# One PSUM region for a unit's scores, one product for the sum of its heads, and the src ids turned and sent by ScalarE

## The chip, the cores and the metric

The kernel runs on one core of one Trainium2 chip. Its time is in device microseconds, the median of several runs; lower is better. A core has five engines with an instruction queue each: PE (TensorE, matrix products, with PEld for the loading of its weights), DVE (VectorE), ACT (ScalarE), POOL (GpSimd) and SP (SyncE, which here only issues transfers). Each engine works through its own queue in order, and semaphores make an instruction wait for another engine or for a transfer.

## What is computed

One attention layer over a graph of 12,500 nodes and 412,500 edges, with residual and two layer norms. Cut to what matters:

```
h, q, k, v = x @ Wn + bn, x @ Wq + bq, x @ Wk + bk, x @ Wv + bv      # 12500 x 128
eh     = edge_attr @ We + be                                          # 412500 x 128
hmid   = leaky_relu(concat(q[src], k[dst], eh) @ A1 + b1, 0.2)        # 412500 x 128
scores = leaky_relu(hmid @ A2 + b2, 0.2)                              # 412500 x 8 heads
w      = softmax(scores.mean(axis=-1), axis=0)                        # over all edges
out    = segment_sum(w[:, None] * v[dst], src, 12500)
y      = layer_norm(h + out) * gamma + beta
result = layer_norm(x + y)
```

The edges come in sorted by dst. So k and v of neighbouring edges lie close together, while q and the sum go by src, which is in no order.

## The kernel before

All is in `sorted_path` (L456). Nodes are cut into blocks of 128, 98 of them, and edges into groups of 1024, 403 of them, which are dealt with in six parts (`CUTS`).

**Making** (`make`, L797, for each part). A group of edges becomes records of 260 floats: the row of v, the part of the hidden layer that comes from dst and from the edge's own attributes, and the src id. PE builds them by one-hot products (L914, L919), ScalarE takes them out of PSUM (L929, L930), and POOL scatters them to DRAM by src block with one indirect DMA per 128 records (L941, 3224 in all) into `rtab`.

**Sums** (`sums_of`, L1072). When a part is made, its records are read back, two src blocks at a time: a **unit**. There are 294, 49 for each part; those of parts 0, 4 and 5 have 12 tiles of 128 records, those of parts 1 to 3 have 14. What one unit goes through, by the functions' names:

- `load` (L1105, SP): the records, `rt`. `load_q` (L1117, SP): q of its two blocks, `qs`.
- `sources` (DVE, L1131): the src id of each record inside its block, `sl`, one column for each tile.
- `turn` (PE, L1139) transposes `sl` into PSUM, so that a tile's ids lie in a row; `turned` (DVE, L1146) takes them out as bytes, `slT`; `put` (L1153, SP) writes them to DRAM as `row`, 1.5 or 1.8 KB; `spread` (L1158, SP) reads them back to all 128 partitions, `rowB`, 192 or 224 KB.
- `onehot` (DVE, L1170): from `rowB` the one-hot matrix `ohT` that picks q. Four tiles are a piece, so this and the next three run three or four times a unit.
- `hidden` (PE, L1184 and L1193): `rt` transposed plus q picked by `ohT`, into PSUM, `ph`. `sloped` (ACT, L1204) writes 0.2 of it to `hm`, and `leaky` (DVE, L1208) the maximum of both.
- `scores` (PE, L1221): hm times A2. A product fills 32 partitions and up to 512 columns: three tiles side by side at 12 tiles, four at 14. Four products fill the four groups of partitions of one PSUM bank, `psc`.
- `above_zero` (ACT, L1235): a ReLU of scores plus b2, from PSUM to `z`, in one piece at 12 tiles and in two at 14. The leaky ReLU of a head is 0.8 of the ReLU plus 0.2 of the linear value; the sum over heads of the linear value is carried by two extra columns of `A2s`, one for its positive and one for its negative part.
- `heads` (PE, L1247): three or four products with `headsum`, which sum the heads of a record into one column for each tile, in `psm`.
- `maxima` (DVE), `maximum` (PE, L1268) and `reference` (DVE, L1276 and L1277): the largest score so far. `weights` (ACT, L1286): the exponentials, `w`, and their sum.
- `select` (DVE, L1295) and `weigh` (ACT, L1309): one-hot of src times w, `ohw`; `add` (PE, L1338): the sum by src; `total` (DVE, L1354): the earlier parts' sum, rescaled, plus this one; `lowered` (ACT, L1328 and L1331) keeps the reference; `store` (SP) writes it.

**What sets the order.** Nothing is reordered by a compiler. `lags` (L1044) and, for the last part, `last_lags` (L1060) give each function a step, as an offset from its unit's first product:

```
turned=-turn + 1 + e, spread=-turn + 3 + 2 * e, q=-9, onehot=-1 - e, sloped=1,
leaky=2, scores=L + 1, above=L + 2 + e, heads=L + 3 + 2 * e, maxima=f, maximum=f + 1,
```

L is twice the number of pieces. `do` files each function under its step, so that several units are in flight at once, and the loop at the end of `sorted_path` deals the steps of part p-1's units out evenly among the making of part p. The last part's units have nothing to be mixed with and run alone behind the making, from about 4440 us; the two layer norms (`closing`) follow from about 4840 us.

**Buffers.** `psc` has one PSUM bank, which the turned ids and the scores of all units take in turn (in the last part the ids have a bank of their own, `late["turn"]`). `z` has one buffer. A hardware DMA takes one of eight semaphores in turn, over all engines that issue any, and first waits for the DMA eight before it.

Of the kernel before, what the change touches and what calls it, by code (L numbers as in the profile page):

```python
# [455 lines left out]
def sorted_path(  # L456
# [39 lines left out]
    A2s = const.tile([D, 32], FP)  # L496
    nc.vector.memset(A2s, 0.0)
    nc.scalar.dma_start(out=A2s[:, :H], in_=A2)
    nc.vector.tensor_reduce(A2s[:, H : H + 1], A2s[:, :H], AX.X, ALU.add)
    for j, part in enumerate((1.0, -1.0)):  # L500
        nc.vector.tensor_scalar(
            A2s[:, H + 1 + j : H + 2 + j], A2s[:, H : H + 1], part * SLOPE / (1 - SLOPE), None,
            op0=ALU.mult,
        )
    nc.vector.memset(A2s[:, H : H + 1], 0.0)
    b2_r = const.tile([1, 32], FP)
    nc.vector.memset(b2_r, 0.0)
    nc.scalar.dma_start(out=b2_r[:, :H], in_=b2.rearrange("h o -> o h"))
    nc.vector.tensor_reduce(b2_r[:, H : H + 1], b2_r[:, :H], AX.X, ALU.add)
    for j, part in enumerate((1.0, -1.0)):  # L510
        nc.vector.tensor_scalar(
            b2_r[:, H + 1 + j : H + 2 + j], b2_r[:, H : H + 1], part * SLOPE / (1 - SLOPE), None,
            op0=ALU.mult,
        )
    nc.vector.memset(b2_r[:, H : H + 1], 0.0)
    b2_d = dram.tile([32, 1], FP, name="b2_d")
    nc.scalar.dma_start(out=b2_d.rearrange("h o -> o h"), in_=b2_r)
    b2_c = const.tile([P, 1], FP)
    headsum = const.tile([P, 4], FP)
    nc.vector.memset(headsum, 0.0)  # L520
    signs = const.tile([32, 1], FP)
    nc.gpsimd.memset(signs, 1 - SLOPE)
    nc.gpsimd.affine_select(
        out=signs, in_=signs, compare_op=ALU.not_equal, fill=SLOPE - 1, base=-(H + 2),
        pattern=[[0, 1]], channel_multiplier=1,
    )
    for j in range(4):
        nc.scalar.dma_start(out=b2_c[32 * j : 32 * j + 32, :], in_=b2_d)
        nc.vector.tensor_copy(headsum[32 * j : 32 * j + 32, j : j + 1], signs)
# [237 lines left out]
    zp_ = pool("z", 1)  # L767
# [6 lines left out]
    pscp = pool("psc", 1, space=PSUM)  # L774
# [269 lines left out]
    def lags(p, nk):  # L1044
# [3 lines left out]
        if p == NP - 1:  # L1048
# [5 lines left out]
            leaky=2, scores=L + 1, above=L + 2 + e, heads=L + 3 + 2 * e, maxima=f, maximum=f + 1,  # L1054
# [5 lines left out]
    def last_lags(nk):  # L1060
# [6 lines left out]
            heads=L + 5, maxima=f, maximum=f + 1, reference=f + 2 + e, weights=f + 3 + e,  # L1067
# [4 lines left out]
    def sums_of(bp):  # L1072
# [63 lines left out]
        def turn(i):  # L1136
            st, nt = state[i], plans[i][0]
            st["pT"] = late.get("turn", pscp).tile([P, 4 * P], FP, name="psc")
            nc.tensor.matmul(  # L1139
                st["pT"][:nt, :P], st["sl"][:, :nt], identB, start=True, stop=True  # L1140
            )

        def turned(i):
            st, nt = state[i], plans[i][0]
            st["slT"] = scp.tile([TM, P], U8, name="slT")
            nc.vector.tensor_scalar(  # L1146
                st["slT"][:nt, :], st.pop("pT")[:nt, :P], 0.0, None, op0=ALU.max
            )

        def put(i):  # L1150
            st, nt = state[i], plans[i][0]
            st["row"] = srow.tile([TM, P], U8, name="row")
            nc.sync.dma_start(out=st["row"][:nt, :], in_=st.pop("slT")[:nt, :])  # L1153

        def spread(i):
            st, nt = state[i], plans[i][0]
            st["rowB"] = late.get("row", rowp).tile([P, TM * P], U8, name="rowB")
            nc.sync.dma_start(  # L1158
# [52 lines left out]
        def slices(m):  # L1211
            sw = -(-m // 4)
            return sw, [(j, min(sw, m - j)) for j in range(0, m, sw)]

        def scores(i, t0, m):
            st = state[i]
            sw, sl = slices(m)
            hm = st["hm"].pop(t0)
            psc = pscp.tile([P, 4 * P], FP, name="psc")
            for q, (j, n) in enumerate(sl):  # L1220
                nc.tensor.matmul(  # L1221
                    psc[32 * q : 32 * q + 32, : n * P], A2s, hm[:, j * P : (j + n) * P],
                    start=True, stop=True,
                )
            full = sum(n == sw for _, n in sl)
            st["z"] = psc, [(0, 32 * full, sw)] + [
                (32 * q, 32 * q + 32, n) for q, (_, n) in enumerate(sl) if q >= full
            ]

        def above_zero(i):  # L1230
            st = state[i]
            psc, pieces = st["z"]
            st["z"] = z = zp_.tile([P, 4 * P], FP, name="z")
            for p0, p1, n in pieces:
                nc.scalar.activation(  # L1235
                    z[p0:p1, : n * P], psc[p0:p1, : n * P], AF.Relu, bias=b2_c[p0:p1, :]
                )

        def heads(i, t0, m):
            st = state[i]  # L1240
            sw, sl = slices(m)
            if t0 == 0:
                st["psS"] = psmp.tile([P, 4 * P], FP, name="psm")
            z = st.pop("z")
            for j in range(sw):
                nv = sum(n > j for _, n in sl)
                nc.tensor.matmul(  # L1247
                    st["psS"][:, t0 + j : t0 + j + (nv - 1) * sw + 1 : sw],
                    z[: 32 * nv, j * P : (j + 1) * P], headsum[: 32 * nv, :nv],
                    start=True, stop=True,  # L1250
                )
# [613 lines left out]
```

## Time and profile before

| | |
|---|---|
| median of 3 runs | 4985.54 us (4974.44 to 4991.73) |
| the profiled execution: its time, its span | 4977.97 us, 4976.3 us |
| PE, products (and weight loads) | 4076.9 us, 82% (64%) |
| DVE | 4181.3 us, 84% |
| ACT | 3168.0 us, 64% |
| POOL | 3327.3 us, 67% |
| DMA | 1462.23 MB, mean 294 GB/s |
| scatters of records (POOL L941) | 3224, 3242.7 us |
| granted TensorE clock, mean | 0.93 |

The busy shares are means over three very different stretches: making with sums (up to about 4440 us, its pace set by different engines early and late), the last part's sums alone, and the layer norms. PE and DVE are both over 80% busy and neither is so all the time, so a row of busy time says little by itself; what an engine waited for, inside one stretch, says more. In a row of a group the figures before the bar are the shape and the count, then come the busy time and the mean length in ns, then the idle time of that engine just before such an instruction and what ended it. In a row of waits stand the idle time, the number of waits and the longest one. In a row of the timeline stand the start, the length, the engine, the line and the operation.

### The profile page before, as it was taken

The page shows a single profiled execution, that of the slowest core. Times are in us where ns is not written, and L with a number is a line of the kernel's source. Part 1 is how long each engine was busy: PE and PEld are TensorE (multiplying, and loading weights), DVE is VectorE, ACT ScalarE, POOL GpSimd, SP SyncE. Part 2 cuts the span into 40 slices and gives each one's busy share as a digit, 9 for nine tenths or more (in the row PEclk, how much of TensorE's full clock was granted, in tenths as well). Part 3 has the DMA queues.
Part 4 walks back from the last instruction along what each step waited for, and adds up shares of the span by engine and source line. Part 5 has one row for each costly group of instructions (what it writes and reads, how often), then busy time and mean ns, then how long its engine had stood idle before and what let it go on. Part 6 is the DMA issues. An engine that isn't in the chain of part 4 may idle for free. (4 is left out here: it accounts for less than half of the span.)

```text
span 4976.3 us, 87101 instructions
## 1 busy us (share of the span) xinstructions
PE 4076.9 (82%) x27267; PEld 3176.9 (64%) x27568; DVE 4181.3 (84%) x9010; ACT 3168.0 (64%) x8326; POOL 3327.3 (67%) x3280
## 2 busy tenths in 40 slices
PE   3665547878888989988988888988889888889997
PEld 2444435666666766776766676776667666666786
DVE  7888867888888888888988887888889898877777
ACT  2442224655656777777777776777777666667785
POOL 3777777777777777777777777767667777731003
PEclk7787868999999999999999999999999999999999
DMA  5888978999888998888898888888888898889864
GB/s 187 285 288 272 369 246 300 317 318 307 275 280 295 315 310 308 311 307 299 315 308 310 303 310 280 306 303 307 297 297 302 300 312 304 298 289 308 302 238 171
DMA packets 603263, 1462.23 MB, mean 294 GB/s; under 512 B 103678, under 2 KB 329105, under 8 KB 600996
## 3 DMA queue, kind: packets, MB, share of 16 engines
q1 hardware_dynamic: 447696, 1027.15, 62.9%
q0 software_dynamic: 154752, 429.39, 22.7%
q8 instruction: 220, 3.60, 0.3%
q14 instruction: 255, 2.09, 0.1%
q10 hardware_dynamic: 340, 0.01, 0.0%
HBM read 884.13 MB, written 585.06 MB: 295 GB/s over the span
## 5 line engine op out<-in xcount | busy, mean ns | idle before, releaser
L941 POOL DMA_INDIRECT rtab<-rec,idx x3224 | 3242.7, 1006 | 1150.6 <-issue 783.3
L929 ACT ACTIVATE rec<-pkv 128x1024 f32<-128x1024 f32 x806 | 821.6, 1019 | 1162.7 <-PE pkv L919 519.1
L1309 ACT ACTIVATE ohw<-ohs,w 128x128 f32<-128x128 bf16 x3822 | 1256.1, 399 | 121.8 <-DVE ohs L1295 59.0
L1338 PE MATMUL psm<-rt,ohw 128*128 128x128 f32 x7644 | 1085.4, 285 | 3.4 <-ACT ohw L1309 0.8
L1338 PEld LDWEIGHTS psm<-rt,ohw 128*128 128x128 f32 x7644 | 997.7, 197 | 101.4 <-ACT hm L1204 13.0
L919 PE MATMUL pkv<-WeS,eat 128*128 128x256 f32 x3224 | 920.5, 412 | 0.0
L1208 DVE TENSOR_TENSOR hm<-ph,hm 128x512 f32<-128x512 f32 (+1 forms) x1029 | 662.5, 644 | 265.9 <-ACT hm L1204 261.2
L914 PE MATMUL pkv<-kvs,ohd 128*128 128x256 bf16 x3224 | 530.0, 291 | 290.5 <-ACT rec L929 283.0
L1184 PE MATMUL ph<-ident,rt 128*128 128x128 f32 x3822 | 625.4, 284 | 118.1 <-DVE hm L1208 112.9
L1170 DVE TENSOR_SCALAR ohT<-rowB,iotaP,power 128x512 bf16<-128x512 uint8 (+2 forms) x1176 | 598.0, 519 | 93.0 <-DMA rowB<-row 92.7
L914 PEld LDWEIGHTS <-ohd 128*128 128x128 bf16 x3224 | 317.0, 103 | 540.6 <-issue 423.4
L919 PEld LDWEIGHTS pkv<-WeS,eat 128*128 128x128 f32 x3224 | 606.4, 209 | 70.2
L1184 PEld LDWEIGHTS ph<-ident,rt 128*128 128x128 f32 x3822 | 442.2, 146 | 323.9 <-issue 144.9
L1204 ACT ACTIVATE hm<-ph 128x512 f32<-128x512 f32 (+1 forms) x1029 | 567.0, 551 | 33.8 <-PE ph L1193 26.8
L857 DVE TENSOR_SCALAR ohd<-dstb,node 128x1152 bf16<-128x1152 uint8 x404 | 564.9, 1398 | 0.0
L1193 PE MATMUL ph<-ohT,qs 128*128 128x512 bf16 (+2 forms) x2051 | 531.6, 340 | 29.2 <-DVE ohT L1170 14.5
L883 DVE TENSOR_TENSOR ats<-pc,oh 128x792 f32<-128x792 f32 x403 | 391.1, 970 | 37.1 <-PE pc L865 37.1
L1221 PE MATMUL psc<-hm,A2s 128*32 128x384 f32 (+2 forms) x2352 | 360.0, 550 | 63.1 <-DVE hm L1208 34.4
L1295 DVE TENSOR_TENSOR ohs<-iotaE,sl 128x512 bf16<-128x512 bf16 (+1 forms) x1029 | 409.1, 398 | 1.0 <-ACT ohw L1309 1.0
L847 DVE TENSOR_REDUCE few<-oh 128x99 bf16<-128x792 bf16 x403 | 395.1, 980 | 13.9
L894 DVE TENSOR_REDUCE pos<-ats 128x8 f32<-128x792 f32 x403 | 389.1, 966 | 1.7
L1247 PE MATMUL psm<-headsum,z 128*128 128x4 f32 (+1 forms) x2058 | 256.7, 245 | 58.0 <-DVE part L1354 50.8
(192 smaller groups left out, 3876.2 us busy)
## 6 DMA issues: line engine op xcount, KB each, us to landing
rt<-rtab SPq DMA_DIRECT2D x147, 1820.0 KB
rt<-rtab SPq DMA_DIRECT2D x147, 1560.0 KB
eat<-in_ea SPq DMA_DIRECT2D x201, 512.0 KB
rtab<-rec,idx POOLq DMA_INDIRECT x3224
dstb<-dtab SPq DMA_DIRECT2D x201, 256.0 KB
rtab<-empty SPq DMA_DIRECT2D x76, 520.0 KB
qs<-qtab SPq DMA_DIRECT2D x294, 128.0 KB
atab<-part SPq DMA_DIRECT2D x294, 128.0 KB
```

Source lines behind the costliest of these rows:

```text
L857: nc.vector.tensor_scalar(to, ids[:, cols], node, None, op0=ALU.is_equal)
L914: nc.tensor.matmul(pk[:, i, h, :], ohd[t], kvs, start=(h == 0), stop=False,)
L919: nc.tensor.matmul(pk[:, i, :, :D], eat[:, (j + i) * P : (j + i + 1) * P], WeS, start=False, stop=True,)
L929: nc.scalar.activation(rec[:, :, :, : 2 * D], pk, AF.Copy)
L941: one_tile = nc.gpsimd.indirect_dma_start(out=rtab[p % TABS][:, :], out_offset=bass.IndirectOffsetOnAxis(ap=idxs[g][:, t : t + 1], axis=0) ...
L1170: nc.vector.tensor_scalar(st["oh"][k][:, (a - t0) * P : (b - t0) * P], st["rowB"][:, a * P : b * P], iotaP, power[:, bs[u] : bs[u] + 1], o ...
L1184: nc.tensor.matmul(ph[:, j * P : (j + 1) * P], st["rt"][:, t0 + j, :D], ident, is_transpose=True, start=(j == 0), stop=False,)
L1193: nc.tensor.matmul(ph[:, cols], st["qs"][:, j0 // t, s, :], oh[:, cols], start=False, stop=(s == 1 and j1 == t0 + n),)
L1204: nc.scalar.activation(hm, state[i]["ph", k][:, : n * P], AF.Copy, scale=SLOPE)
L1208: nc.vector.tensor_tensor(hm, ph[:, : n * P], hm, op=ALU.max)
L1309: nc.scalar.activation(ohw[:, j, :], ohs[:, :, j], AF.Copy, scale=st["w"][:, t0 + j : t0 + j + 1])
L1338: nc.tensor.matmul(st["psS"][:, (1 + u) * P : (2 + u) * P], ohw[:, j, :], st["rt"][:, t0 + j, D : 2 * D], start=(k == 0), stop=(k == t - 1),)
```

## The change

Three things are rewritten; the loop, the tables and the rest stay.

**Scores.** One static PSUM bank `mix` of 512 columns takes the place of the bank `psc`. Columns 0 to 127 and 128 to 255 are two boxes, for even and odd units; columns 256 to 383 take the turned ids; the end of the kernel uses columns 256 to 511 once. A product now multiplies one tile: tile t goes to partition group t mod 4, and inside the group its eight heads go to the rows 8 (t div 4) and on, because `A2s` has four copies that are shifted by eight columns. The three or four products of one group add into the same box. So all scores of a unit are 128 x 128 numbers, in place of 128 x 384 or 128 x 512. That makes 12 or 14 products of 128 columns where four products of 384 or 512 columns stood (three of 512 and one of 256 at 14 tiles).

**Leaky ReLU and heads.** The columns for the linear part are gone. ScalarE writes 0.2 (scores + b2) to `z` in one piece (L1216), a new step `peak` on DVE takes the maximum of that and scores + b2 (L1222), and one product with a block matrix `headsum` of 16 columns sums the heads of all tiles (L1231). `z` is 128 x 128 and has two buffers. `peak` stands one step after `above`.

**Src ids.** `turned` is an activation on ScalarE instead of an operation of DVE (L1138), and `put` and `spread` are issued by ScalarE instead of SP (L1143, L1148). Their steps are the same.

```diff
-    A2s = const.tile([D, 32], FP)
+    A2s = const.tile([D, 4, 32], FP)
     nc.vector.memset(A2s, 0.0)
-    nc.scalar.dma_start(out=A2s[:, :H], in_=A2)
...
+    nc.scalar.dma_start(out=A2s[:, 0, :H], in_=A2)
...
+    for q in range(1, 4):
+        nc.vector.tensor_copy(A2s[:, q, q * H : (q + 1) * H], A2s[:, 0, :H])
+        nc.vector.tensor_copy(b2_r[:, q, :], b2_r[:, 0, :])
...
+    nc.vector.tensor_scalar(b2_c[:, 1:2], b2_c[:, 0:1], SLOPE, None, op0=ALU.mult)
...
+    headsum = const.tile([P, 4, 4], FP)
...
-    zp_ = pool("z", 1)
+    zp_ = pool("z", 2)
...
-    pscp = pool("psc", 1, space=PSUM)
+    mixp = pool("mix", 1, space=PSUM)
+    mix = mixp.tile([P, 4 * P], FP, name="mix")
...
-            leaky=2, scores=L + 1, above=L + 2 + e, heads=L + 3 + 2 * e, maxima=f, maximum=f + 1,
+            leaky=2, scores=L + 1, above=L + 2 + e, peak=L + 3 + e, heads=L + 3 + 2 * e, maxima=f, maximum=f + 1,
...
-            heads=L + 5, maxima=f, maximum=f + 1, reference=f + 2 + e, weights=f + 3 + e,
+            peak=L + 4, heads=L + 5, maxima=f, maximum=f + 1, reference=f + 2 + e, weights=f + 3 + e,
...
         def turn(i):
             st, nt = state[i], plans[i][0]
-            st["pT"] = late.get("turn", pscp).tile([P, 4 * P], FP, name="psc")
+            st["pT"] = mix[:, 2 * P : 3 * P]
...
         def turned(i):
...
-            nc.vector.tensor_scalar(
-                st["slT"][:nt, :], st.pop("pT")[:nt, :P], 0.0, None, op0=ALU.max
-            )
+            nc.scalar.activation(st["slT"][:nt, :], st.pop("pT")[:nt, :P], AF.Relu)
...
-            nc.sync.dma_start(out=st["row"][:nt, :], in_=st.pop("slT")[:nt, :])
+            nc.scalar.dma_start(out=st["row"][:nt, :], in_=st.pop("slT")[:nt, :])
...
-            nc.sync.dma_start(
+            nc.scalar.dma_start(
                 out=st["rowB"][:, : nt * P],
...
+        def box(i):
+            return mix[:, i % 2 * P : (i % 2 + 1) * P]
...
+        def scores(i):
+            nt, hm = plans[i][0], state[i].pop("hm")[0]
+            for t in range(nt):
+                q, s = divmod(t, 4)
                 nc.tensor.matmul(
-                    psc[32 * q : 32 * q + 32, : n * P], A2s, hm[:, j * P : (j + n) * P],
-                    start=True, stop=True,
-                )
+                    box(i)[32 * s : 32 * s + 32, :], A2s[:, q, :], hm[:, t * P : (t + 1) * P],
+                    start=(q == 0), stop=(t + 4 >= nt),
+                )
...
         def above_zero(i):
...
+            st["z"] = zp_.tile([P, P], FP, name="z")
+            nc.scalar.activation(
+                st["z"][:r, :], box(i)[:r, :], AF.Identity, bias=b2_c[:r, 1:2], scale=SLOPE
+            )
+
+        def peak(i):
+            st, r = state[i], 32 * min(4, plans[i][0])
+            nc.vector.scalar_tensor_tensor(
+                st["z"][:r, :], box(i)[:r, :], b2_c[:r, 0:1], st["z"][:r, :],
+                op0=ALU.add, op1=ALU.max,
+            )
...
+            nc.tensor.matmul(
+                st["psS"][:, :nt], st.pop("z")[:r, :], headsum[:r, :nt], start=True, stop=True
+            )
...
-            do(s0 + o["scores"], scores, i, 0, nt)
+            do(s0 + o["scores"], scores, i)
             do(s0 + o["above"], above_zero, i)
-            do(s0 + o["heads"], heads, i, 0, nt)
+            do(s0 + o["peak"], peak, i)
+            do(s0 + o["heads"], heads, i)
```

How the instructions stand. First ScalarE in the last stretch, where the last part's units run alone; one unit's round, before:

```order
L1286 ACTIVATE w,sums<-S,ref 128x12
L1309 ACTIVATE ohw<-ohs,w 128x128 x4
L1235 ACTIVATE z<-psc,b_c 128x384
L1204 ACTIVATE hm<-ph 128x512
L1309 ACTIVATE ohw<-ohs,w 128x128 x4
L1204 ACTIVATE hm<-ph 128x512
L1328 ACTIVATE by<-refs,ref 128x2
L1331 ACTIVATE refs<-ref 128x2
L1309 ACTIVATE ohw<-ohs,w 128x128 x4
L1204 ACTIVATE hm<-ph 128x512
```

and with the change:

```order
L1138 ACTIVATE slT<-mix 12x128
L1143 DMA row<-slT 12x128
L1268 ACTIVATE w,sums<-S,ref 128x12
L1291 ACTIVATE ohw<-ohs,w 128x128 x4
L1216 ACTIVATE z<-mix,b_c 128x128
L1194 ACTIVATE hm<-ph 128x512
L1291 ACTIVATE ohw<-ohs,w 128x128 x4
L1148 DMA rowB<-row 128x1536
L1194 ACTIVATE hm<-ph 128x512
L1310 ACTIVATE by<-refs,ref 128x2
L1313 ACTIVATE refs<-ref 128x2
L1291 ACTIVATE ohw<-ohs,w 128x128 x4
```

The ids and their put come in right ahead of the weights w, and the spread stands two pieces of ohw, the z and one sloped copy behind the put; z itself stands where it stood.

Second DVE in the same stretch, before:

```order
L1276 TENSOR_REDUCE m_58512<-psm 128x1
L1277 SCALAR_TENSOR_TENSOR ref<-m_58512,ref 128x1
L1170 TENSOR_SCALAR ohT<-rowB,iotaP,power 128x512
L1146 TENSOR_SCALAR slT<-psc 12x128
L1208 TENSOR_TENSOR hm<-ph,hm 128x512
L1295 TENSOR_TENSOR ohs<-iotaE,sl 128x512
L1131 SCALAR_TENSOR_TENSOR sl<-mask,rt 128x12
L1354 SCALAR_TENSOR_TENSOR part<-old,by,psm 128x128 x2
L1170 TENSOR_SCALAR ohT<-rowB,iotaP,power 128x512
```

and with the change:

```order
L1258 TENSOR_REDUCE m_60244<-psm 128x1
L1259 SCALAR_TENSOR_TENSOR ref<-m_60244,ref 128x1
L1160 TENSOR_SCALAR ohT<-rowB,iotaP,power 128x512
L1198 TENSOR_TENSOR hm<-ph,hm 128x512
L1277 TENSOR_TENSOR ohs<-iotaE,sl 128x512
L1123 SCALAR_TENSOR_TENSOR sl<-mask,rt 128x12
L1336 SCALAR_TENSOR_TENSOR part<-old,by,psm 128x128 x2
L1222 SCALAR_TENSOR_TENSOR z<-mix,b_c,z 128x128
L1160 TENSOR_SCALAR ohT<-rowB,iotaP,power 128x512
```

The turned ids have left the place ahead of the leaky maximum of a piece, and the maximum of the scores has come in between the sum of a unit and the one-hot of the next piece.

Third PE in the same stretch, before:

```order
L1338 MATMUL psm<-rt,ohw 128x128 x4
L1247 MATMUL psm<-headsum,z 128x4 x3
L1184 MATMUL ph<-ident,rt 128x128 x4
L1193 LDWEIGHTS qs
L1193 MATMUL ph<-ohT,qs 128x512
L1193 LDWEIGHTS qs
L1193 MATMUL ph<-ohT,qs 128x512
L1139 LDWEIGHTS sl
L1139 MATMUL psc<-identB,sl 12x128
L1338 MATMUL psm<-rt,ohw 128x128 x4
L1221 MATMUL psc<-hm,A2s 32x384 x4
L1268 MATMUL psm<-ident,mx 128x128
```

and with the change:

```order
L1320 MATMUL psm<-rt,ohw 128x128 x4
L1231 MATMUL psm<-headsum,z 128x12
L1174 MATMUL ph<-ident,rt 128x128 x4
L1183 LDWEIGHTS qs
L1183 MATMUL ph<-ohT,qs 128x512
L1183 LDWEIGHTS qs
L1183 MATMUL ph<-ohT,qs 128x512
L1131 LDWEIGHTS sl
L1131 MATMUL mix<-identB,sl 12x128
L1320 MATMUL psm<-rt,ohw 128x128 x4
L1208 MATMUL mix<-hm,A2s 32x128 x12
L1250 MATMUL psm<-ident,mx 128x128
```

Twelve short products stand where four long ones stood, and one where three stood; both keep their places between the same neighbours.

85 lines of the change are left out of this document (21 added, 64 removed).

## The prediction

> **What bounds the kernel now.** I read the page's time slices first, then busy time by stretch, then the waits of each engine inside those stretches, and last a timeline of the final stretch. The time slices show the same mix for most of the run, so the question is which engine sets the pace in which part. Busy time by stretch, with the timeline row of one scatter below it:
>
> ```profile
> core 0: us, PE busy (x) PEld busy (x) DVE busy (x) ACT busy (x) POOL busy (x), PEclk, DMA share, GB/s
> 1500.00:3000.00 1500.00, 1326.19 (x9111) 1042.10 (x9210) 1319.89 (x2792) 1083.19 (x2873) 1148.63 (x1154) 0.96 0.89 309
> 3100.00:4400.00 1300.00, 1153.92 (x8070) 906.65 (x8165) 1129.69 (x2478) 931.58 (x2529) 917.27 (x924) 0.96 0.88 303
> 4450.00:4830.00 380.00, 356.76 (x2778) 280.38 (x2826) 295.51 (x828) 299.58 (x929) 27.46 (x13) 1.00 0.84 288
> ...
> 2501.35 0.96 POOL L941 DMA_INDIRECT rtab<-rec,idx  x1 [0.30 <-issue]
> ```
>
> A scatter holds POOL for 0.96 us and 0.30 us pass before the next: 1.26 us. In the first stretch 1154 of them make 1454 of 1500 us, so **POOL sets the pace there at 97%** and no other engine's work is worth much. In the second 924 make 1164 of 1300 us (90%): POOL waits for others. In the third it has no scatters left and **PE is busy for 357 of 380 us**. What the engines wait for in the second stretch and, after the mark, in the third:
>
> ```profile
> DVE hm L1208 <- ACT hm L1204: 69.9, 67, 2.6
> DVE sl L1131 <- DMA rt<-rtab: 41.9, 32, 3.8
> DVE ohT L1170 <- DMA rowB<-row: 25.7, 19, 3.0
> SPq L1158 <- DMA row<-slT: 358.9, 90, 8.9
> ...
> PE psc L1221 <- DVE hm L1208: 17.0, 13, 1.6
> PE ph L1193 <- DVE ohT L1170: 3.4, 6, 1.2
> ACT w L1286 <- DVE ref L1277: 70.8, 46, 3.3
> ```
>
> In the second stretch DVE works 1130 of 1300 us, and 138 of its 170 idle us are the first three rows: ScalarE's sloped copy, the records of a unit, the spread src ids. I take **DVE, held up by those three, as its bound**. The fourth row is the queue of SP: after the put it stands about 4 us (358.9 over 90) until the row has landed, before it may issue the spread and everything behind it. In the third stretch PE waits for almost nothing, and ScalarE stands 1.5 us a unit before w (70.8 over 46).
>
> **The change, part by part.** PE, sum of heads. Rows of the third stretch; the first column is the start:
>
> ```profile
> 4580.63 1.05 PE L1338 MATMUL psm<-rt,ohw 128*128 128x128 f32 x8
> 4581.52 0.73 PE L1247 MATMUL psm<-headsum,z 128*128 128x4 f32 x6
> 4582.11 0.63 PE L1184 MATMUL ph<-ident,rt 128*128 128x128 f32 x4
> ...
> 4584.34 0.85 PE L1221 MATMUL psc<-hm,A2s 128*32 128x384 f32 x8
> 4585.12 0.49 PE L1268 MATMUL psm<-ident,mx 128*128 128x128 f32 x2
> ```
>
> Six records go from 4581.52 to the next start at 4582.11: 0.59 us, 0.098 each. A unit of 12 tiles keeps two of six: -0.39 us. A unit of 14 had eight and keeps two: -0.59 us.
>
> PE, scores. Eight records take 4584.34 to 4585.12, 0.78 us, and twelve or fourteen products of 128 columns (24 or 28 records) take their place. The columns streamed into each of the four groups of output partitions stay 384 (512 in two groups at 14 tiles), and the eight records now overlap four deep: mean 517 ns each, below, would make 4.1 us in a row. Lower bound 0, since the streams are the same. Upper bound: each record pays the pace of L1338 above, eight in 0.89 us or 0.111 each, so 24 x 0.111 = 2.67 us, +1.89 us a unit. I take +0.10 us, near the lower end, because the groups stay distinct from one product to the next and the row nearest in shape is L1221 itself.
>
> The other durations, from the groups of instructions kept apart by shape:
>
> ```profile
> L1221 PE MATMUL psc<-hm,A2s 128*32 128x384 f32 x1176 | 160.9, 517 | 46.9 <-DVE hm L1208 23.8 <-DVE slT L1146 23.0
> L1235 ACT ACTIVATE z<-psc,b_c 96x512 f32<-96x512 f32 x147 | 98.1, 667 | 0.5 <-PE psc L1221 0.5
> L1235 ACT ACTIVATE z<-psc,b_c 32x256 f32<-32x256 f32 x147 | 68.5, 466 | 1.9
> L1235 ACT ACTIVATE z<-psc,b_c 128x384 f32<-128x384 f32 x147 | 82.4, 561 | 0.0
> L1309 ACT ACTIVATE ohw<-ohs,w 128x128 f32<-128x128 bf16 x3822 | 1256.1, 399 | 121.8 <-DVE ohs L1295 59.0 <-DVE S L1257 39.7 <-PE pkv L914 9.2
> L1331 ACT ACTIVATE refs<-ref 128x2 f32<-128x2 f32 x294 | 59.5, 202 | 7.8
> L1354 DVE SCALAR_TENSOR_TENSOR part<-old,by,psm 128x128 f32<-128x128 f32 x490 | 146.1, 338 | 20.5 <-PE psm L1338 19.3 <-PE pc L865 0.9
> L1146 DVE TENSOR_SCALAR slT<-psc 12x128 uint8<-12x128 f32 x147 | 39.9, 271 | 0.0
> ...
> L1153 SPq DMA_DIRECT2D row<-slT x294: 315/362/794, 765.3 to 4810.9; - x147
> L1158 SPq DMA_DIRECT2D rowB<-row x294: 319/320/782, 769.1 to 4812.2; - x147
> ```
>
> ScalarE. The new z is one 128x128 piece with one pointer operand, like L1309: 399 ns. It replaces 667 + 466 = 1133 ns at 14 tiles, 561 ns at 12. The turned ids (128 columns, few rows) lie between L1331's 202 and L1309's 399 ns; I take 300. Both issues come over from SP at 362 and 320 ns. Together: 14 tiles -734 + 300 + 682 = +0.25 us; 12 tiles -162 + 982 = +0.82 us. It is the one engine with over a quarter idle in the first two stretches. In the third the ids and their put stand right ahead of w, where it waits 1.5 us a unit anyway; that wait hides the put there, and without it the unit would grow by the 0.82 us. The put also waits for its own activation to end, the spread for the put's landing; queued behind the spread are the sloped copy (L1204), so DVE's leaky step, so PE.
>
> DVE. The leaky maximum (one 128x128 pass with a PSUM operand, like L1354) adds 338 ns, the turned ids take 271 away: +0.07 us. It also waits for z, with the whole DVE queue behind it. In these rows of the third stretch z ends at 4580.93, and DVE has finished the instruction ahead of the new place by then:
>
> ```profile
> 4580.27 0.58 DVE L1354 SCALAR_TENSOR_TENSOR part<-old,by,psm 128x128 f32<-128x128 f32 x2
> 4580.37 0.56 ACT L1235 ACTIVATE z<-psc,b_c 128x384 f32<-128x384 f32 x1
> 4580.79 0.53 DVE L1170 TENSOR_SCALAR ohT<-rowB,iotaP,power 128x512 bf16<-128x512 uint8 x1
> ```
>
> The shorter z would end at about 4580.77, so DVE, free at 4580.85, waits for nothing there; bounds 0 and the 0.3 us of a z that comes a piece late. I take 0.1 us a unit for the second stretch. The product behind it must start at 4581.52: 0.34 us after 4580.85 is 4581.19, in time.
>
> The two transfers. SP loses 588 issues and the 4 us wait behind each put. The spread now goes out when ScalarE arrives at it. In the trace, SP's rows for one unit are:
>
> ```profile
> 2510.32 0.36 SPq L1153 DMA_DIRECT2D row<-slT  x1
> 2510.73 0.39 SPq L1120 DMA_DIRECT2D qs<-qtab  x1
> ...
> 2517.68 0.32 SPq L1158 DMA_DIRECT2D rowB<-row  x1
> 2518.09 0.39 SPq L1109 DMA_DIRECT2D rt<-rtab  x1
> ```
>
> A put of 1.8 KB and the spread lie 7.4 us apart, on the queue that also carries the 1820 KB loads of rt. I take it that the small put waits behind larger transfers of its queue and lands sooner on a queue of its own, in about 2.5 us; bounds: the 4 us and more that SP waits now, and the 1.6 us between b_d's issue (4.66) and b_c's (6.24) on ScalarE's queue in the idle start:
>
> ```profile
> 4.66 0.23 ACTq L517 DMA_DIRECT2D b_d<-b_r  x1
> 6.24 1.76 ACTq L528 DMA_DIRECT2D b_c<-b_d  x4
> ```
>
> [...]
>
> **The sum**, against the profiled execution (span 4976.3 us, time 4977.97 us). Up to 3000 us: 0, POOL hides all of it; at best the 46 us by which the stretch is over POOL's pace. Second stretch, 93 units, DVE as bound: half of the 25.7 us for rowB saved (-13), a third of the 41.9 us for rt because SP is no longer held (-14), +0.07 x 93 = +6 for the maximum, +0.1 x 93 = +9 for its wait. ScalarE's mean +0.5 us a unit reaches DVE only where the sloped copy is late; a quarter of the 46 us is +11. PE's 0.4 us a unit counts little while DVE is ahead of it: a fourth of 37, -9. Sum -10, bounds -60 (all DMA waits and PE's share) and +90. Third stretch, 46 units: -0.39 + 0.10 = -0.29 us each, -13, and the 3.4 us that PE waits on late ohT: -17; bounds -25 and +87 (1.89 x 46). The start differs by a few constants: 0. Together **-27 us: 4951 us profiled**. The median of the runs shown, 4985.5, lies 7.6 us over the profiled time; predicted median 4959 us.
>
> **Rivals.** *A, larger gain*: DVE loses both DMA waits of the second stretch and POOL runs at its full pace before it. For: SP spends its time in just these waits. Against: DMA is 88% busy either way. -60 - 20 - 17 = about -95, 4890 us. *B, ScalarE becomes the bound of the last stretch*: 299.6 + 46 x 0.82 = 337 us busy, and if its 70.8 us before w stay, 408 us against 380: +28. Against: the put lies in that very wait. With the second stretch at -10: +18, about 5004 us; half as strong it is no change. *C, slower: ScalarE stands at the spread.* If the put lands no sooner than now, ScalarE reaches the spread some 3 us behind it (rec, w, four ohw) and stands up to 4 us, with the sloped copy behind. It decides from a landing time of about 3.5 us on. At 1.5 us a unit over some 190 units, 285 us of ScalarE; with a third of it passing to DVE and POOL, +95, less the -17 of the last stretch and without the -13: about 5070 us. *D, the scores run one after another*: +1.89 us a unit where PE or DVE binds, 139 units, with half of it absorbed in the second stretch: 88 there and 87 in the third, beside the forecast's -10, -18 (heads) and -3: +144, about 5130 us. [...]
>
> **How the numbers follow.** This kernel can be told from no change at about 0.3%, 15 us. Chances: forecast 0.40, A 0.13, B 0.19, C 0.22, D 0.06. Of the forecast's 0.40 I count 0.33 as faster by over 15 us and 0.07 within; B gives 0.10 within and 0.09 slower. Faster 0.33 + 0.13 = 0.46, same 0.17, slower 0.09 + 0.22 + 0.06 = 0.37. The forecast's own range is 4930 to 4985; with most of A, B and C it is 4895 to 5075, leaving out the far ends of A and C and all of D.
>
> **What would show it.** Right: PE's heads at 588 records, the scores of a unit still done in about 0.9 us from start to start, DVE's wait for rowB in the second stretch about halved (25.7 us now), the last stretch shorter by 10 to 20 us, POOL's scatters at 1.26 us before 3000 us. Wrong: ScalarE's queue waiting for row<-slT by more than 100 us; DVE's wait for ACT hm or for z growing by more than it loses for rowB; w no longer waiting in the last stretch while PE does; scatters further apart before 3000 us.

## The result and the profile after

The changed kernel takes **4937.42 us** in the median of 3 runs (4934.47 to 4943.84), the kernel before 4985.54 (4974.44 to 4991.73): ratio 0.992, 95% interval 0.9902 to 0.9938. The profiled execution took 4934.47 us with a span of 4932.7 us, 43.6 us less than the span before. The forecast was 4959 us, 27 us less than before.

Where the 43.6 us went shows in stages. They are cut at the last scatter of a part and at the weights w of the 251st and of the last unit, all times from the two traces, in us:

| stage | before | changed | difference | forecast |
|---|---|---|---|---|
| start and making of parts 1 to 4 | 3024.7 | 3015.7 | -9.0 | 0 |
| making of the fifth part | 718.3 | 682.3 | -36.0 | -10 for both |
| making of the sixth part | 652.4 | 657.8 | +5.4 | |
| last scatter to w of unit 251 | 96.2 | 97.9 | +1.7 | |
| w of unit 251 to w of unit 294 (43 units) | 344.8 | 341.2 | -3.6 | -17 for 46 units |
| the rest | 139.8 | 137.8 | -2.0 | 0 |

So the size came out between the forecast and rival A, and from another place than forecast: the fifth part gave more, the last stretch next to nothing. Busy time of the changed kernel by stretch (the third and second row answer to the ones shown of before; the stretches begin and end a little earlier, as the kernel does):

```profile
core 0: us, PE busy (x) PEld busy (x) DVE busy (x) ACT busy (x) POOL busy (x), PEclk, DMA share, GB/s
1500.00:3000.00 1500.00, 1249.45 (x10495) 1032.41 (x10592) 1331.99 (x2803) 1022.22 (x2888) 1146.74 (x1159) 0.97 0.90 310
3100.00:4360.00 1260.00, 1085.79 (x9216) 889.47 (x9309) 1129.66 (x2460) 885.05 (x2549) 906.71 (x918) 0.97 0.91 310
4410.00:4790.00 380.00, 343.84 (x3367) 283.52 (x3412) 300.99 (x837) 303.71 (x982) 27.64 (x13) 0.99 0.83 286
```

In the second row DVE does 1129.7 us of work in 1260 us; before it did as much in 1300. The prediction took it as the bound; it now idles 130 instead of 170 us. What DVE and PE wait for in that stretch:

```profile
DVE ohT L1160 <- DMA rowB<-row: 53.4, 29, 3.8
PEld psm L1231 <- DVE z L1222: 41.7, 46, 3.5
DVE z L1222 <- ACT z L1216: 32.4, 29, 3.1
DVE hm L1198 <- ACT hm L1194: 11.6, 22, 1.7
DVE sl L1123 <- DMA rt<-rtab: 9.0, 12, 1.3
```

DVE's wait for the sloped copy fell from 69.9 to 11.6 us and the one for the records from 41.9 to 9.0; the one for rowB doubled, from 25.7 to 53.4, and the new wait for z takes 32.4. In the last stretch (4410 to 4790 us) stands:

```profile
PEld mix L1208 <- DVE hm L1198: 40.1, 38, 3.1
PE mix L1208 <- DVE hm L1198: 29.3, 22, 2.9
ACT hm L1194 <- DMA row<-slT: 28.6, 19, 2.5
DVE hm L1198 <- ACT hm L1194: 20.2, 21, 2.3
ACT w L1268 <- DVE ref L1259: 13.6, 25, 1.0
```

ScalarE now stands 28.6 us at the spread until the row has landed (the wait is put down to the sloped copy behind it), and hardly before w: 13.6 us, where it was 70.8. PE waits 29.3 us for the last leaky maximum ahead of the scores, where it waited 17.0. One such stand in ScalarE's own timeline:

```profile
4593.74 0.41 ACT L1291 ACTIVATE ohw<-ohs,w 128x128 f32<-128x128 bf16 x1
4595.40 0.36 ACTq L1148 DMA_DIRECT2D rowB<-row  x1
4595.81 0.60 ACT L1194 ACTIVATE hm<-ph 128x512 f32<-128x512 f32 x1 [1.67 <-DMA row<-slT]
```

The products themselves, on PE: twelve for the scores, in a piece of 16 records and one of 8, then, four steps later, the one that sums the heads:

```profile
4612.90 0.65 PE L1208 MATMUL mix<-hm,A2s 128*32 128x128 f32 x16
4613.88 0.43 PE L1208 MATMUL mix<-hm,A2s 128*32 128x128 f32 x8 [0.33 <-DVE hm L1198]
4614.23 0.49 PE L1250 MATMUL psm<-ident,mx 128*128 128x128 f32 x2
...
4618.16 0.39 PE L1231 MATMUL psm<-headsum,z 128*128 128x12 f32 x2
4618.40 0.63 PE L1174 MATMUL ph<-ident,rt 128*128 128x128 f32 x4
```

The heads take 0.24 us from start to start where they took 0.59. Over all units in which nothing is waited for (the lower quartile at full clock), 24 records of the scores take 0.79 us and 28 take 1.00, against 0.78 and 0.99 for eight before.

How the src ids travel can be followed for each unit in the traces: a transfer has landed at the last update of its semaphore before the next transfer takes that semaphore. Means for a unit behind 3100 us, in the making of the fifth and sixth part, in us (the third column is a variant of the experiments below):

| | before | changed | changed, both issues on SP (e11) |
|---|---|---|---|
| from the put's issue to its landing | 5.6 | 4.5 | 6.7 |
| from there to the spread's issue | 0.1 | 0.7 | 0.1 |
| from the spread's issue to its landing | 4.6 | 6.2 | 4.6 |
| from `sources` on DVE to `rowB` landed | 18.8 | 19.1 | 19.0 |

So in the making the put does land sooner on ScalarE's queue, but the spread takes longer, and `rowB` is there no sooner. In 32 of 92 units of the changed kernel SP had issued a load of records less than 2 us ahead of the spread; these spreads took 7.8 us, the others 5.4, and these units hold 42.5 of the 55.8 us that DVE idles ahead of a unit's first one-hot. With the issues on SP the spread goes out ahead of the load, and there is one such unit. In the last stretch the put lands later than before: after 4.2 us in the mean, against 2.5 before and 3.0 in e11.

### The profile page after: what moved, and what is told of

The parts are those of the page before. It is cut to its first block, busy times and chain, and to the rows that moved or that the text cites. A ratio compares the mean times of both kernels' runs of the same rounds, so it can differ in the third digit from the quotient of the medians.

```text
span 4932.7 us, 94669 instructions
## 1 busy us (share of the span) xinstructions
PE 3888.2 (79%) x31093; PEld 3151.9 (64%) x31390; DVE 4200.4 (85%) x9003; ACT 3058.9 (62%) x8473; POOL 3313.5 (67%) x3281
## 5 line engine op out<-in xcount | busy, mean ns | idle before, releaser
L1320 PE MATMUL psm<-rt,ohw 128*128 128x128 f32 x7644 | 1082.4, 284 | 25.4 <-ACT ohw L1291 22.8
L1320 PEld LDWEIGHTS psm<-rt,ohw 128*128 128x128 f32 x7644 | 994.0, 196 | 125.2 <-ACT ohw L1291 31.6
L1174 PE MATMUL ph<-ident,rt 128*128 128x128 f32 x3822 | 623.3, 283 | 133.4 <-DVE hm L1198 128.8
L1174 PEld LDWEIGHTS ph<-ident,rt 128*128 128x128 f32 x3822 | 440.0, 145 | 264.8 <-DVE hm L1198 104.6
L1208 PE MATMUL mix<-hm,A2s 128*32 128x128 f32 x7644 | 308.3, 282 | 86.6 <-DVE hm L1198 77.1
L1208 PEld LDWEIGHTS mix<-hm,A2s 128*32 128x32 f32 x7644 | 202.4, 111 | 150.2 <-DVE hm L1198 101.5
```

Of the source, the lines that this page charges most:

```text
L1174: nc.tensor.matmul(ph[:, j * P : (j + 1) * P], st["rt"][:, t0 + j, :D], ident, is_transpose=True, start=(j == 0), stop=False,)
L1320: nc.tensor.matmul(st["psS"][:, (1 + u) * P : (2 + u) * P], ohw[:, j, :], st["rt"][:, t0 + j, D : 2 * D], start=(k == 0), stop=(k == t - 1),)
```

## The experiments

Twelve runs of eight kernels were made, on four chips, and the chips were not alike. On two of them the kernel *before* took 5887.89 and 5840.97 us, with a mean granted clock of 0.86 to 0.88 in the traces made there instead of 0.93. These are called the throttled chips below; the name says what the clock showed, not why they were slower. Every ratio is to runs of the kernel before on the same chip, but a ratio from a throttled chip is not to be laid beside one from the others; the making is about a fifth longer there, while the last stretch of the same kernel differs by 6 us at most (granted clock in that stretch 0.97 to 1.00 on the throttled chips). Times of stages are those of one trace each; the changed kernel's making, traced three times (c0 and e5 below have the same), took 4355 to 4362 us, its fifth part 681 to 692.

**Halves of the change.** First the ids alone, on the kernel before:

```diff
-            nc.vector.tensor_scalar(
-                st["slT"][:nt, :], st.pop("pT")[:nt, :P], 0.0, None, op0=ALU.max
-            )
+            nc.scalar.activation(st["slT"][:nt, :], st.pop("pT")[:nt, :P], AF.Relu)
...
-            nc.sync.dma_start(out=st["row"][:nt, :], in_=st.pop("slT")[:nt, :])
+            nc.scalar.dma_start(out=st["row"][:nt, :], in_=st.pop("slT")[:nt, :])
...
-            nc.sync.dma_start(
+            nc.scalar.dma_start(
                 out=st["rowB"][:, : nt * P],
```

> The kernel before, with only the src ids changed: turned by ScalarE, put and spread issued by ScalarE; scores, z and heads are those of before. Theory (both halves of the change gain, about equally): about -20 us on before, ratio 0.996; the making of the fifth part gets 10 to 20 us shorter and the last stretch does not gain. Rival S (the scores, z and heads carry the whole gain): no change, 0.998 to 1.002, or slower by up to 20 us, because ScalarE still has the long z and now stands at the spread. Rival I (the transfers carry the whole gain): about 0.990.

Measured on a throttled chip: 5895.2 us, ratio 1.0006 (0.9989 to 1.0024). The last stretch's 43 units took 349.3 us, 4.5 more than before the change. The 20 us that the theory gave to the ids are not seen there. Again, on a second throttled chip:

> e1_ids_only once more (the kernel before with the src ids turned and sent by ScalarE), if possible on a chip like the first. Theory: the transfers' place gives nothing by itself, because ScalarE has the long z beside them: ratio 0.998 to 1.003, with the making of the fifth part (719 us before, 682 with the change) at 710 to 725. Rival (the wait of SP behind each put is what made the fifth part slow): ratio 0.992 to 0.996, the fifth part below 695 us.

5829.37 us, ratio 0.9981 (0.9966 to 0.9996), last stretch 350.9 us. The fifth part, 815.4 us there, cannot be held against the bounds named, which were for the other chips. The ids alone were never run on an unthrottled chip.

Second the scores alone: the changed kernel with the three places above put back (DVE turns, SP sends).

> The changed kernel with the src ids as before: turned by DVE, put and spread issued by SP; scores, z, maximum and heads are those of the change. Theory: about -25 us on before, ratio 0.995, and the last stretch gains some 10 us more than in the changed kernel, because nothing stands at the spread there. Rival S: 0.990 or less. Rival I: 0.998 to 1.002.

5975.9 us on the same throttled chip as the first: ratio 1.0149 (1.0129 to 1.0169). Slower by 1.5%, which none of the theories had. Two repeats:

> e2_scores_only once more (the changed kernel with the ids turned by DVE and sent by SP). Theory (scores, z, maximum and heads carry the gain): ratio 0.989 to 0.993, the fifth part 675 to 695 us, the last stretch shorter than in the changed kernel by some 5 us (in e2 its 43 units took 339 us). Rival: ratio 0.997 or more, the fifth part above 705 us.

> e2_scores_only again (scores, z, maximum and heads of the change; ids turned by DVE and sent by SP as before), for a chip like the first. On such a chip, theory (the scores carry the gain of the fifth part, the ids that of the last stretch): ratio 0.992 to 0.995, the fifth part 680 to 695 us (before 718, with the change 682), the last stretch's 43 units 338 to 340 us. Rival (the transfers carry the fifth part): fifth part 705 us or more, ratio above 0.996. On a chip that throttles as the third does: 1.012 to 1.016 again.

The second, on the other throttled chip: 5912.91 us, 1.0123 (1.0096 to 1.0151). The third, on an unthrottled one: 4979.91 us, **0.999** (0.9975 to 1.0004), the fifth part 705.6 us, the last stretch 336.2. So on a chip like the first the scores gain some 9 us in the last stretch and nothing that can be told in the making: the theory that they carry the gain is wrong, and the rival that the transfers carry the fifth part holds by its bounds (705 us, 0.996), the first of them narrowly. Why the making does not gain, in this run, 3030 to 4360 us:

```profile
PEld psm L1233 <- DVE z L1224: 74.8, 49, 8.4
DVE sl L1123 <- DMA rt<-rtab: 58.8, 35, 6.8
DVE ohT L1162 <- DMA rowB<-row: 32.9, 24, 5.3
DVE z L1224 <- ACT z L1218: 30.0, 23, 2.4
DVE hm L1200 <- ACT hm L1196: 5.4, 10, 0.9
```

The scores take DVE's wait for the sloped copy away, 66.9 us before to 5.4 in the same window; z is now 0.35 us on ScalarE where it was 1.13 us in two pieces for a unit of 14 tiles. DVE runs into the next two instead: the records (48.9 us before, 58.8 here), and z.

**The place of the transfers.** The changed kernel with both issues on SP again, the ids still turned by ScalarE:

```diff
-            nc.scalar.dma_start(out=st["row"][:nt, :], in_=st.pop("slT")[:nt, :])
+            nc.sync.dma_start(out=st["row"][:nt, :], in_=st.pop("slT")[:nt, :])
...
-            nc.scalar.dma_start(
+            nc.sync.dma_start(
                 out=st["rowB"][:, : nt * P],
```

> The changed kernel with put and spread issued by SP again; ScalarE still turns out the ids. Theory (the transfers' place makes about half of the gain, the turned ids next to nothing): as e2, about 0.995; DVE's waits for rt and rowB in the making of the fifth part come back to about 30 us each. Rival (the ids' operation leaving DVE is what helps): as the changed kernel, 0.991.

> e3_issues_on_sp again (the changed kernel with put and spread issued by SP, the ids still turned by ScalarE), for a chip like the first. Theory: the last stretch's 43 units 322 us as in e3 and e5; the making as in the changed kernel or up to 10 us longer; so 4920 to 4932 us, ratio 0.987 to 0.990, within 6 us of e5. Rival (the transfers' place shortens the making): fifth part above 700 us and the whole not below the changed kernel's 4940 us. On a chip that throttles as the third does: 1.010 to 1.014 again, below e10 by 5 to 15 us.

Throttled: 5966.0 us, 1.0134 (1.0114 to 1.0155). Unthrottled, beside the scores alone: 4955.96 us, **0.9937** (0.9918 to 0.9956), 24 us below the scores alone on the same chip, for one operation of 0.25 us that went from DVE to ScalarE. The last stretch is 327.2 us (321.8 in the throttled run), the fifth part 702.8: above the 700 us that the rival named, and 20 us above the changed kernel's. The theory's making within 10 us of the changed kernel's, and its 0.987 to 0.990, are missed. DVE's waits, 3030 to 4360 us:

```profile
DVE sl L1123 <- DMA rt<-rtab: 62.9, 36, 7.0
DVE ohT L1160 <- DMA rowB<-row: 30.9, 24, 5.1
```

those of SP's queue in the same kernel and stretch:

```profile
SPq L1148 <- DMA row<-slT: 495.7, 93, 10.9
SPq L1143 <- ACT slT L1138: 183.7, 47, 8.8
```

and DVE's of the changed kernel, where SP has no put or spread to wait at:

```profile
DVE ohT L1160 <- DMA rowB<-row: 60.9, 32, 4.6
DVE sl L1123 <- DMA rt<-rtab: 13.1, 14, 2.9
```

With the issues on SP its queue stands 496 us behind the puts, and the loads of records behind them come late: 63 us of DVE's time. With the issues on ScalarE the records are in time (DVE reaches `sources` 2.8 us after they landed in the mean, against 0.9) and the wait for `rowB` grows instead: +30 for -50 us. The table of the result shows what that growth is not: ScalarE reaches the spread 0.7 us after the row landed, and as late in the units where DVE then waits (0.72) as in the others (0.75). It goes with the loads of records, which SP, free of the puts, now issues just ahead of the spread. In the fifth and sixth part together the trade is worth 17 to 27 us, by the three traces of that making against e11's one.

**The changed kernel again**, to know what the throttled chips had done:

> The changed kernel itself, unaltered, once more, because the four runs ahead were made on a chip that grants TensorE half its clock for about 1,500 of 5,900 us, where the first pair of traces has 700 of 4,960. If the granted clock decides what the change is worth: on that chip the change is slower than before, ratio 1.012 to 1.020 (e2 to e4 stood at 1.013 to 1.018); on a chip like the first, 0.990 to 0.994. If it does not, 0.992 on either, and the variants e2 to e4 are slower by what they alter.

4941.86 us, ratio 0.9929 (0.9901 to 0.9956), on an unthrottled chip; stages within 1.5 us of the first trace. So the expectation for a chip like the first is met; the one for a throttled chip was not put to the test with this kernel. The nearest to it, next, was run there.

**The last stretch.** One step later for the spread there, `spread=-turn + 6` in place of `+ 5` in `last_lags`:

> The changed kernel with the spread one step later in the last stretch only. Theory (ScalarE's 28.6 us before the sloped copy in the last stretch are its stand at the spread until the row has landed): most of the 28.6 us go, the last stretch gets 5 to 15 us shorter, ratio to before about 0.990. Rival (DVE's wait for rowB takes its place, or PE bounds the stretch anyway): the same time as the changed kernel within 3 us.

5996.25 us on a throttled chip, 1.0183 (1.0163 to 1.0203). The stand for the row is gone (3.1 us in three waits from 5510 to 5870 us), and the 43 units took 345.8 us, no less than the changed kernel's 341.2. DVE's wait for rowB, 4.5 us in the changed kernel, grew:

```profile
DVE ohT L1160 <- DMA rowB<-row: 13.8, 19, 1.6
ACT ohw L1291 <- DMA row<-slT: 3.1, 3, 1.2
```

So taking the stand away in this manner gains nothing, much as the rival had it. Taking both issues off ScalarE there does gain:

```diff
-            nc.scalar.dma_start(out=st["row"][:nt, :], in_=st.pop("slT")[:nt, :])
+            (nc.sync if late else nc.scalar).dma_start(out=st["row"][:nt, :], in_=st.pop("slT")[:nt, :])
...
-            nc.scalar.dma_start(
+            (nc.sync if late else nc.scalar).dma_start(
                 out=st["rowB"][:, : nt * P],
```

> The changed kernel with put and spread issued by SP for the units of the last stretch only, and by ScalarE before. Theory (ScalarE's stand at the spread sets the pace of the last stretch): the last stretch, 49 units, 15 to 22 us shorter than in the changed kernel (in e3, with SP for all units, 43 of them took 322 us, in the changed kernel 341), the rest unchanged. Rival (that gain of e3 came from the whole run, not from that stretch): within 3 us of the changed kernel.

**4925.4 us**, ratio 0.9886 (0.9866 to 0.9906), beside the unaltered change at 4941.86 on the same chip: the best version. Its 43 units took 321.8 us, 19.5 less. That is the size the theory gave, though e4 speaks against its cause; DVE's larger wait for rowB does not account for e4, since it is nearly as large here. The medians differ by 16.5 us, less than the stretch gave; in the traces the fifth part took 691.7 us here and 680.8 in the unaltered change, with the same instructions. PE waits less for the last leaky maximum (4450 to 4790 us; the changed kernel on the same chip had 32.4):

```profile
PEld mix L1208 <- DVE hm L1198: 16.4, 13, 2.0
DVE ohT L1160 <- DMA rowB<-row: 11.6, 11, 1.9
DVE hm L1198 <- ACT hm L1194: 0.4, 1, 0.4
```

Then the scores one step later as well, `scores=L + 2` in `last_lags`:

> e5_sp_in_last with the scores of the last stretch one step later. Theory (PE, which waits 16.7 us there for the last leaky maximum ahead of the scores, has other products to do meanwhile): that wait below 5 us, the last stretch 8 to 15 us shorter than in e5, ratio to before 0.986. Rival (z and its maximum then come late, and PE stands before the heads as long as it stood before the scores): the same as e5 within 3 us, or slower.

On a throttled chip 5897.06 us, 1.0106 (1.0067 to 1.0145); the 43 units took 321.5 us against 321.8: the rival. PE's wait before the scores stayed (15.2 us).

**Why short products are no dearer.** The same products in another order:

```diff
-            for t in range(nt):
+            for t in sorted(range(nt), key=lambda t: t % 4):
```

> The changed kernel with the same products of the scores, sorted by their group of output partitions, so that the three or four that add into one group stand behind each other instead of four groups in turn. Theory (what keeps 24 short products as cheap as 8 long ones is that neighbours go to different groups and run side by side): 2 to 2.7 us for a unit's scores where the changed kernel takes 0.79, PE 1.2 to 1.9 us a unit more, the last stretch 50 to 90 us longer and the whole 60 to 150 us. Rival (short products cost their streams and no more in any order): 0.8 us, no difference.

The lower quartile of the scores went to 1.52 us for 24 records and 1.96 for 28, twice the changed kernel's 0.79 and 1.00. So the order matters, by less than the 2 to 2.7 us expected of a unit and the 50 to 90 us of the last stretch. The time is 5945.97 us, 1.0178 (1.0150 to 1.0207), 33 us above the scores alone on that chip (which differ from it in the ids too), and the 43 units took 357.3 us, 16 more; PE's added 0.73 us a unit (31 us) passes on by half. A unit's scores of this order, and what comes next:

```profile
5615.75 1.59 PE L1208 MATMUL mix<-hm,A2s 128*32 128x128 f32 x24
5617.27 0.49 PE L1250 MATMUL psm<-ident,mx 128*128 128x128 f32 x2
```

This order also puts products that add into the same rows behind each other. That this, and not the shared group, is what costs is unlikely by rows of the same kernel: records of L1174, which fill all partitions and go to different columns, start 109 ns apart in the median at full clock, those of L1320, which add into the same columns, 112.

Where neighbours go to different groups of partitions, as in the changed kernel, three times the records took 0.01 us more for a unit (0.79 us for 24 against 0.78 for 8).

## Why the prediction was right, and where it was not

The changed kernel is faster, as forecast, by 48 us in the medians where 27 were forecast. That the number came so near is in part luck: the second stretch gave three times what was forecast, the last a fifth of it, and the terms of the second were wrong in both directions.

- **What bounds the kernel**: borne out for both stretches of the kernel before behind 3000 us. DVE's work in the second is unchanged and its idle time shrank by the 40 us. But work that leaves DVE does not shorten that stretch in full: from e10 to e11 some 25 us of it left (0.271 us for each of 93 units), and the fifth and sixth part got 8 us shorter. "Up to 3000 us: 0" missed 9 us, inside the 46 that it allowed.
- **PE's products**: heads -0.35 us a unit of 12 (forecast -0.39); scores +0.01 at either size (forecast +0.10, bounds 0 and 1.89). Rival D is out, and e9 shows what it would have needed: neighbours in one group; even then +0.73 us a unit of 12 tiles, not +1.89.
- **ScalarE's and DVE's durations**: in the profile's groups z takes 347 ns (forecast 399) and the maximum 347 (338); the turned ids 250 (300):

```profile
L1216 ACT ACTIVATE z<-mix,b_c 128x128 f32<-128x128 f32 x294 | 102.1, 347 | 0.5 <-ACT slT L1138 0.4
L1222 DVE SCALAR_TENSOR_TENSOR z<-mix,b_c,z 128x128 f32<-128x128 f32 x294 | 101.9, 347 | 134.2 <-ACT z L1216 128.2 <-PE mix L1131 2.8 <-ACT slT L1138 1.3
L1138 ACT ACTIVATE slT<-mix 12x128 uint8<-12x128 f32 x147 | 36.8, 251 | 8.8 <-PE mix L1208 8.8
```

- **The second stretch, forecast -10, measured about -31 (fifth and sixth part)**. The sum for the transfers was -27 (13 for rowB and 14 for rt); e11 against the changed kernel's making puts them at -17 to -27 (702.8 + 662.1 against 682.3 + 657.8 in the first trace, 691.7 + 656.0 in e5's). But both terms were wrong in themselves: rowB lost 28 us where 13 were to be saved, and rt saved 33 where 14 were. The step that failed is the one from "the small put ... lands sooner on a queue of its own, in about 2.5 us" to half of the wait for rowB saved; the 2.5 us were an estimate of the author's, which no run shows in the making. The put did land sooner, after 4.5 us against 5.6 before and 6.7 in e11, though not after 2.5; but the spread itself then took 6.2 us where it had taken 4.6, a time that the sum left as it was. The other failed term is +11 for "ScalarE's mean +0.5 us a unit reaches DVE": DVE's wait for the sloped copy fell by 58 us, and e10, with the short z and without the ids, shows that the shorter z brought it. The new wait for z, 32.4 us, was +9 in the sum.
- **The turned ids** were booked as 271 ns that DVE saves in the second stretch, 25 us in 93 units, hidden in a term of +0.07 beside the maximum. From e10 to e11, on one chip, they gave 24 us, but elsewhere: by one trace each some 10 in the first parts and 9 in the last stretch, where the sum had nothing for them, and 8 in the fifth and sixth.
- **The last stretch, forecast -17, measured -3.6 in 43 units**. PE's saving was there: the scores alone gave -9, the turned ids another -9 to -14 (327.2 and 321.8 against 336.2). The sentence that failed is "that wait hides the put there": with both issues on ScalarE 14 to 19.5 us came back (341.2 and 341.3 against 327.2 and 321.8). That is rival B's mechanism, ScalarE's added work reaching PE, with rival C's beside it: the put landed after 4.2 us there, over the 3.5 that C named, and ScalarE stood 28.6 us at the spread with the sloped copy behind. Of the signs named, one of being wrong came true, w no longer waiting while PE does; and DVE's wait for rowB, which was to be halved, doubled. ScalarE's idle time at the row stayed below the 100 us named: 40 us in the whole run by the profile's waits. In numbers: both issues take 0.67 us of ScalarE a unit (medians of 0.32 and 0.35 over 294), 29 us in 43 units, and its wait before w went from 70.8 to 13.6 us, so the cover was used up. That it is the issue time rather than the stand is argued from e4 (stand gone, no gain, on a throttled chip) and e5 (both gone, 19.5 us gained), not shown by itself.
- **Rival C** was right about the place and wrong about the price: the put lands after 4.2 to 4.5 us, over its 3.5, and ScalarE stands at the spread, 28.6 us in the last stretch, but not 285 over the run; and taking the stand away as e4 does gains nothing.

What the transfers' move brought is thus mixed: the put landed sooner from ScalarE's queue in the making (4.5 us against 5.6 and 6.7), but not in the last stretch (4.2 against 2.5 and 3.0), and `rowB` came no sooner (19.1 us after `sources` against 18.8). The issues themselves are the smaller part of what SP was freed of: 0.68 us a unit, 63 us in the second stretch, beside 359 us of standing behind the puts.

## What to carry to other kernels

When a transfer waits on its queue for another's landing, look at what stands behind it there: with the issues on SP (e11) its queue stood 496 us behind the puts from 3030 to 4360 us, and DVE waited 63 us for the loads of records behind them; with the issues on ScalarE it waited 13. So move such a transfer where less is waiting, stage by stage: here ScalarE was the better issuer while DVE was the bound (the fifth part 681 to 692 us against 703) and the worse one when PE was (341 us for 43 units against 322 to 327). Look too at what the freed queue then issues: here the spread took 6.2 us in the making instead of 4.6, and 7.8 where a load of records had gone out less than 2 us ahead of it, against 5.4 elsewhere. Here short products that go to different groups of output partitions in turn cost what the long ones cost (0.79 us against 0.78), and the same products in another order cost twice that (1.52). And repeat a one-per-cent result on another chip before it is believed: the kernel of e3 and e11 took 1.0134 of the time before on one chip and 0.9937 on another.

## What the runs showed of the hardware

**A small gain on one chip was a loss on another.** The changed kernel with its issues on SP stood at 0.9937 on one chip and at 1.0134 on a throttled one, the scores alone at 0.999 and at 1.0123 and 1.0149. The same program before takes 4982.82 and 4989.97 us on two chips and 5887.89 and 5840.97 on two others. Busy time from 1800 to 3600 us there (PE, PEld, DVE, ACT, POOL, then granted clock, DMA share, GB/s). The ids alone, on the first throttled chip:

```profile
1800.00:3600.00 1800.00, 1430.91 (x8705) 1090.68 (x8798) 1251.01 (x2568) 1064.25 (x2840) 1093.53 (x1099) 0.89 0.72 244
```

the scores alone, on the same chip:

```profile
1800.00:3600.00 1800.00, 1382.69 (x9694) 1082.08 (x9785) 1259.80 (x2683) 929.38 (x2587) 1046.35 (x1066) 0.86 0.71 237
```

the scores by group, on the second:

```profile
1800.00:3600.00 1800.00, 1434.28 (x9957) 1149.91 (x9952) 1262.30 (x2630) 966.96 (x2717) 1068.76 (x1085) 0.90 0.71 241
```

POOL is 58 to 61% busy there, against 77% from 1500 to 3000 us in the first trace of the kernel before, so its pace no longer covers the parts that it set. PE has less to do with the new scores, and it is granted less clock, 0.86 against 0.89; with the scores by group, which keep it busy longer, 0.90. Over the whole run the granted clock is 0.871 and 0.869 with the ids alone, 0.856 and 0.861 with the scores alone, 0.883 with the scores by group. In the first traces of the kernel before and of the changed kernel the clock is either full or half, and a stretch of half clock lasts 5.6 and 6.2 us in the mean. In the kernel before, the longest gap of PE in the 8 us ahead of such a stretch is 2.2 us in the median, against some 0.8 us ahead of places drawn at random. So half clock goes with gaps of PE there; what sets the clock was not shown. That the lower clock is why the scores lose 1.2 to 1.5% on the throttled chips was not tested, and two things speak against the clock as the whole cause: the scores by group have the highest clock there and still lose 1.8%, and the clock cannot account for the kernel before being 900 us longer there. The ids alone, which take as long and have a clock of 0.871, spend 1520 us at half clock, worked out from that mean with full and half as the only two; the kernel before spent 698 on the first chip. At half speed the 820 us more cost 410 at most, an estimate that takes PE for the bound throughout. What makes PE wait there in the first place stays open.
